# A four-layer transformer block on one core: the sums over a head taken for two states at once on four column tiles, and the decay's second product on two row tiles

## The chip, the core and the metric

The kernel runs on one core of a Trainium2 chip. The metric is the device time in microseconds (us) of one execution, the median of several. Five engines work side by side, each through its own instructions in order: PE (TensorE, the matrix engine, with its weight loads shown apart as PEld), DVE (VectorE), ACT (ScalarE), POOL (GpSimd) and SP (SyncE, which here only issues DMAs). An instruction waits on semaphores for what it needs, and what stands behind it on the same engine waits with it.

## The reference

The input is 32 sequences of 64 tokens with 256 features. Four layers follow each other: a transformer layer with self-attention, cross-attention and an MLP; a recurrent layer (layer 1); a layer with two large cross-attentions of 16 heads of 128 features and an MLP; and a last cross-attention layer. Only layer 1 is touched. Cut to what matters, with 32 heads of 8 features (`h`, `s_`):

```python
xm = xa[:, :, None] + sx[:, :, None] * (maa_stack + xxx)
xk, xw, xv, xr, xg = (xm[:, :, j] for j in range(5))
w = jnp.exp(-jnp.exp(time_decay + jnp.tanh(xw @ td_w1) @ td_w2)).reshape(b, l, h, s_)
r, k, v = ...                      # three 256x256 products of xr, xk, xv
def step(s, rkvw):
    r_t, k_t, v_t, w_t = rkvw
    a = k_t[..., :, None] * v_t[..., None, :]
    out = jnp.einsum('bhi,bhij->bhj', r_t, u * a + s)
    s = a + w_t[..., :, None] * s
    return (s, out)
```

The state `s` of a head is an 8x8 matrix that runs over the 64 tokens. `out` sums over the head's 8 rows. The decay `w` comes from two small products: 256 to 64 features (`td_w1`), a tanh, and 64 to 256 features (`td_w2`).

## The kernel before

**Groups and stages.** The 2048 tokens are four groups of 512 (eight sequences each). A group's activations in layer 1 are tiles of 128 partitions x 2 x 512: 256 features as two halves of 128 partitions (`c` = 0, 1), 512 tokens in the free dimension. Every layer is a Python generator which yields between pieces of work; `weave` runs a main generator and pulls lighter ones along at a rate. Layer 1 of group 0 is a main generator, with layer 0 of group 1 and a filler (the products `k2p_f`, `v2p_f` of layer 2) woven in. Layer 1 of groups 1, 2 and 3 is the light generator, each followed by a layer 0 (or layer 3) of another group, woven at rates 1.13 to 1.25 into layer 2 of the group before. The number of yields of layer 1 therefore sets which piece of layer 2 stands beside which piece of what follows layer 1. The framework then puts every engine's instructions in an order of its own by priority, and adds the waits.

**The recurrence.** `states(c, n)` (L552 to L575) makes the products for two of the eight columns `j` of a head's state, for one half `c`: four calls `n` = 0 to 3 take `j` = (0, 2), (4, 6), (1, 3), (5, 7). In it, a 0/1 matrix spreads `v` over the head's rows with two matmuls (L558, output `vj`), which use two row tiles of the PE array (32 input rows each, `m` = j // 2). DVE multiplies by `k` (L567), then runs two scans over the tokens (L573); POOL writes the start values (L563) and multiplies by `r` (L574). The result is `a`, 128 x 2 x 512.

**The sums over a head.** In the loop at L586 each call's `a` is summed by two matmuls with a 0/1 matrix of 32 columns (L596, output `op`), each on a column tile of 32: tile `m` of `op` gets columns `j` = 2m (`q` = 0, `start`) and `j` = 2m + 1 (`q` = 1, `stop`). So `n` = 0 writes column tiles 0 and 1, `n` = 1 tiles 2 and 3, and `n` = 2, 3 add the odd columns to the same tiles. The loop keeps two calls of `states` ahead. After `n` = 3 a matmul `bp` (L603) and two DVE instructions (L604, L605) finish that half. `beside(i)` gives the second and later matmuls of a set a higher priority, so that they stand behind the first one in PE's order.

**The decay.** `dwp` (through `linear`, L165) is the product with `td_w1`, 64 output columns, on partitions 0 to 63; ACT takes the tanh (L505); `wp` (L510) multiplies by `td_w2`, once for each half `c`, from 64 input rows; ACT takes two exponentials for each half (L512, L513).

**Float32 on PE.** All matmuls are float32, and each is two passes in the trace (64 matmuls of `op` are 128 records).

**Buffers.** `bank` is one of four PSUM tiles of 512 columns, `banks` one of two tiles of 1024 columns, used by `vj`, by layer 2's scores `s2p` and layer 0's scores `sp`. The 128 x 2 x 512 tiles come from a pool of 12 (`four`).

Of the kernel before, what the change touches and what calls it, by code (L numbers as in the profile page):

```python
# [10 lines left out]
AF = mybir.ActivationFunctionType  # L11
# [3 lines left out]
P = 128  # L15
# [6 lines left out]
NC = D // P  # L22
# [5 lines left out]
C_ID, C_HB, C_HB8, C_SEL, C_GAT, C_M0, C_M1 = 0, 128, 256, 384, 640, 704, 705  # L28
# [40 lines left out]
def kernel(  # L69
# [16 lines left out]
    V, A, PL, PE = nc.vector, nc.scalar, nc.gpsimd, nc.tensor  # L86
# [8 lines left out]
    def bank(name):  # L95
        return psum1.tile([P, 512], F32, tag="b1", name=name)
# [20 lines left out]
    ct = cp.tile([P, C_N], F32, name="ct")  # L117
# [13 lines left out]
    def vec(name, i=0):  # L131
        at = VAT[name] + i
        return vt[:, at : at + 1]
# [27 lines left out]
    def linear(ps, w, at, step, y, cols=P):  # L161

        for kc in range(NC):
            o = at + kc * step
            PE.matmul(ps, w[:, o : o + cols], y[:, kc, :], start=(kc == 0), stop=(kc == NC - 1))  # L165
# [259 lines left out]
    @contextmanager  # L425
    def beside(i):

        if i:
            with tc.high_priority(offset=4000):
                yield  # L430
        else:
            yield
# [5 lines left out]
    def cbt(ap):  # L438

        return ap.rearrange("p c (b t) -> p (c b) t", b=GB)  # L440
# [7 lines left out]
    def layer1(g, work):  # L448
# [6 lines left out]
        w5, w6 = slot(L1_AT), slot(L1_AT + 1)  # L455
# [11 lines left out]
        ps = bank(f"t5p_{g}")  # L467
        linear(ps, w5, 0, 192, xx)
        A.activation(t5[:, 0, :], ps, AF.Tanh)
        ps = bank(f"t5bp_{g}")  # L470
# [27 lines left out]
        xw, xk = mixed(1, 0)  # L498
        yield
        yield  # L500
        de = big("de")
        dw = de[:64, 0, :]
        ps = bank(f"dwp_{g}")
        linear(ps[:64, :], w5, 384, 64, xw, cols=64)
        A.activation(dw, ps[:64, :], AF.Tanh)  # L505
        ws = big("ws")
        PL.memset(cbt(ws)[:, :, 0:1], 0.0)
        for c in range(NC):
            ps = bank(f"wp_{g}_{c}")
            PE.matmul(ps, w5[:64, 512 + c * P : 512 + (c + 1) * P], dw, start=True, stop=True)  # L510
            e = de[:, 1, :]
            A.activation(e, ps, AF.Exp, bias=vec("L1_xattn_time_decay", c))  # L512
            A.activation(bt(ws[:, c, :])[:, :, 1:], bt(e)[:, :, :-1], AF.Exp, scale=-1.0)  # L513
        yield

# [2 lines left out]
        for f, n, at in ((0, "k", 0), (2, "v", 512)):  # L518
# [7 lines left out]
            for c in range(NC):  # L526
                ps = bank(f"{n}p1_{g}_{c}")
# [22 lines left out]
        def states(c, n):  # L550

            j0 = (0, 4, 1, 5)[n]  # L552
            vj = banks(f"vj_{g}_{c}_{n}")
            for i in range(2):
                m, q = (j0 + 2 * i) // 2, j0 % 2
                rows = slice(32 * m, 32 * m + 32)
                with beside(i):
                    PE.matmul(  # L558
                        vj[:, i, :], ct[rows, C_SEL + q * P : C_SEL + (q + 1) * P], v[rows, c, :],
                        start=True, stop=True,  # L560
                    )
            a = big(f"a{c}{n}")
            PL.tensor_copy(  # L563
                a.rearrange("p i (b t) -> p i b t", b=GB)[:, :, :, 0:1],
                s0t[:, c, j0 : j0 + 3 : 2, g * GB : (g + 1) * GB].unsqueeze(3),
            )
            V.tensor_tensor(  # L567
                a.rearrange("p i (b t) -> p i b t", b=GB)[:, :, :, 1:],
                vj.rearrange("p i (b t) -> p i b t", b=GB)[:, :, :, :-1],
                bt(k[:, c, :])[:, :, :-1].unsqueeze(1).to_broadcast([P, 2, GB, S - 1]), ALU.mult,  # L570
            )
            for i in range(2):
                V.tensor_tensor_scan(a[:, i, :], ws[:, c, :], a[:, i, :], 0.0, ALU.mult, ALU.add)  # L573
            PL.tensor_tensor(a, a, r[:, c : c + 1, :].to_broadcast([P, 2, GT]), ALU.mult)  # L574
            return j0, a  # L575
# [7 lines left out]
        for c in range(NC):  # L583
            V.scalar_tensor_tensor(ruk[:, c, :], r[:, c, :], vec("L1_xattn_u", c), k[:, c, :], ALU.mult, ALU.mult)
        w9 = slot(L1_AT + 4)
        for at, (c, n) in enumerate(todo):  # L586
            if at + 2 < 8:
                ahead.append(states(*todo[at + 2]))
                yield
            if n == 0:  # L590
                op = bank(f"op_{g}_{c}")
            j0, a = ahead.pop(0)
            for i in range(2):
                m, q = (j0 + 2 * i) // 2, j0 % 2
                with beside(i):
                    PE.matmul(  # L596
                        op[32 * m : 32 * m + 32, :], ct[:, C_GAT + 32 * q : C_GAT + 32 * q + 32], a[:, i, :],
                        start=(q == 0), stop=(q == 1),
                    )
            yield  # L600
            if n == 3:
                bp = bank(f"bp_{g}_{c}")
                PE.matmul(bp, hb, ruk[:, c, :], start=True, stop=True)  # L603
                V.tensor_tensor(v[:, c, :], bp, v[:, c, :], ALU.mult)  # L604
                V.tensor_tensor(v[:, c, :], op, v[:, c, :], ALU.add)  # L605
                yield
# [390 lines left out]
def _layout(inputs):  # L997

    import numpy as np

    f = {k: np.asarray(v) for k, v in inputs.items()}
    i = np.arange(D)
    turned = (i // P) * P + (i % 16) * 8 + (i % P) // 16

    def rows(w):

        return w.reshape(-1, P, w.shape[1]).transpose(1, 0, 2).reshape(P, -1)

    def tall(w):

        return np.concatenate([w, np.zeros((P - w.shape[0], w.shape[1]), w.dtype)], 0)

    def slot(*parts):
        w = np.concatenate(parts, 1)
        return np.concatenate([w, np.zeros((P, WSLOT - w.shape[1]), w.dtype)], 1)

    l0 = {k[9:]: v for k, v in f.items() if k.startswith("L0_xattn_")}
    l1 = {k[9:]: v for k, v in f.items() if k.startswith("L1_xattn_")}
    l2 = {k[9:]: v for k, v in f.items() if k.startswith("L2_xattn_")}
    l3 = {k[9:]: v for k, v in f.items() if k.startswith("L3_xattn_")}  # L1020

    def mlp(w1, w2):

        return [slot(rows(w1[:, :512])), slot(rows(w1[:, 512:])), slot(rows(w2[:512])), slot(rows(w2[512:]))]

    qkv, kv = l0["w_qkv"], l0["w_kv"]
    w2 = l1["maa_w2"]
    maa_w1 = np.concatenate([l1["maa_w1"], l1["maa_w1"][:, 128:]], 1)
    slots = [
        slot(rows(qkv[:, :512])),  # L1030
        slot(rows(qkv[:, 512:]), rows(l0["w_ao"])),
        slot(rows(l0["w_q"]), rows(kv[:, :D])),
        slot(rows(kv[:, D:]), rows(l0["w_co"])),
        *mlp(l0["w1"], l0["w2"]),
        slot(rows(maa_w1), rows(l1["td_w1"]), tall(l1["td_w2"])),
        slot(w2[:4].reshape(P, D), tall(np.concatenate([w2[4], w2[4]], 0))),
        slot(rows(l1["Wk"].T), rows(l1["Wv"].T[:, turned])),
        slot(rows(l1["Wr"].T), rows(l1["Wg"].T[:, turned])),
        slot(rows(l1["Wo"].T[turned]), rows(l1["Wfk"].T)),
        slot(rows(l1["Wfr"].T), rows(l1["Wfv"].T)),  # L1040
    ]
    for a in "12":
        for q in range(4):
            at = slice(512 * q, 512 * q + 512)
            slots += [slot(rows(l2[n + a][:, at])) for n in ("wq", "wk", "wv")]
            slots.append(slot(rows(l2["wo" + a][at])))
    slots += mlp(l2["w_fc1"], l2["w_fc2"])
    slots += [
        slot(rows(l3["q_w"]), rows(l3["k_w"])),
        slot(rows(l3["v_w"]), rows(l3["cproj_w"])),  # L1050
        *mlp(l3["fc_w"], l3["proj_w"]),
    ]
    f["L1_xattn_gn_w"] = l1["gn_w"][turned]
    f["L1_xattn_gn_b"] = l1["gn_b"][turned]

    def feature_major(x):

        return x.reshape(G, GT, NC, P).transpose(3, 0, 2, 1)

    def token_major(x):  # L1060

        return x.reshape(G, TT, P, D).transpose(2, 0, 1, 3)

    ctx = f["ctx_2048"]
    arrays = {
        "x": token_major(f["x"]),
        "cT": feature_major(ctx),
        "s0": ctx[:, 2:10].reshape(B, NC, P, 8).transpose(2, 1, 3, 0),
        "m_self": f["mask_1x1xSxS2_fc1"].reshape(S, S),
        "m_cross": f["mask_Bx1xSxS2_ff1"].reshape(B // 2, 2, S, S).transpose(2, 1, 0, 3),  # L1070
        "m_key": np.ascontiguousarray(f["mask_BxS2_bf1"]).view(np.uint8).reshape(B // 2, 2, S).transpose(1, 0, 2),
        "vecs": np.concatenate([f[n].reshape(-1, P).T for n, _ in VECS], 1),
        "brow": np.concatenate([f[n].reshape(-1) for n in ROWS])[None],
        "vrow": np.stack([np.stack([l2[f"b{v}"].reshape(-1), l2[f"bias_v{a}"].reshape(-1)]) for a, v in (("1", "v1"), ("2", "v2"))]),
        "wts": np.stack(slots),
        "cst": _constants(),
    }
    return {k: np.ascontiguousarray(v) for k, v in arrays.items()}
# [27 lines left out]
```

## Time and profile before

| | |
|---|---|
| median of three runs | 2191.03 us (2188.73 to 2194.2) |
| the profiled execution's own time | 2198.33 us |
| its span, from first to last instruction | 2196.6 us |
| mean granted TensorE clock | 0.973 |
| matmul passes / instructions in the trace | 15264 / 36396 |
| DMA | 197.26 MB, mean 90 GB/s |

In the page a line of a group reads: source line, engine, operation, output and inputs by tile name, shape and type, count, then busy time, mean duration of one in ns, and the idle time of the engine just before, with what ended it. Matmuls are pipelined, so that the durations of single passes overlap; what a set of matmuls really occupies is the distance from its start to the start of the next one. The layer 1 recurrences of the four groups lie at about 313 to 426, 573 to 641, 1005 to 1074 and 1444 to 1520 us of the span.

### The profile page before, as it was taken

What the parts mean: (1) busy time and instruction counts of PE and PEld (TensorE: products, weight loads), DVE (VectorE), ACT (ScalarE), POOL (GpSimd) and SP (SyncE); (2) the same over time, 40 slices, a digit from 0 to 9 for tenths busy, and PEclk for the clock granted to TensorE, in tenths of its full rate; (3) what the DMA queues carried; (4) which work ended last, traced back from release to release, by engine and by line L of the source; (5) the groups of instructions that cost most, each with busy time, mean ns of one, the idle gap of its engine ahead of it and who ended that gap; (6) DMA issues with size and microseconds to landing.
All of it is one profiled execution on the core that took longest, in us unless ns stands there. A gap on an engine that the chain in (4) does not pass through costs nothing. (4 is left out here: it accounts for less than half of the span.)

```text
span 2196.6 us, 36396 instructions
## 1 busy us (share of the span) xinstructions
PE 2058.2 (94%) x15264; PEld 1243.4 (57%) x15264; DVE 1156.9 (53%) x1965; ACT 631.8 (29%) x1000; POOL 542.4 (25%) x498
## 2 busy tenths in 40 slices
PE   5989998999989899999898999999999999999998
PEld 3455444464545565655555656555566767566665
DVE  3672668434655747325548573376574366424662
ACT  1222322223232313232313232322323133321441
POOL 2221344113432313123323131243211111100110
PEclk9999998999999999999999999999999999999998
DMA  7233231237312112333121132331312432212010
GB/s 245 95 128 109 93 104 57 99 106 252 112 58 63 58 47 77 95 112 116 49 63 60 50 100 83 117 123 51 89 55 95 128 121 70 94 43 87 25 39 20
DMA packets 79795, 197.26 MB, mean 90 GB/s; under 512 B 9616, under 2 KB 14352, under 8 KB 79632
## 3 DMA queue, kind: packets, MB, share of 16 engines
q1 hardware_dynamic: 77472, 191.88, 27.2%
q8 instruction: 121, 1.98, 0.4%
q0 software_dynamic: 576, 2.10, 0.3%
q10 hardware_dynamic: 1584, 0.95, 0.1%
q14 instruction: 42, 0.34, 0.1%
HBM read 158.98 MB, written 35.91 MB: 89 GB/s over the span
## 5 line engine op out<-in xcount | busy, mean ns | idle before, releaser
L165 PE MATMUL q2p<-h,w 128*128 128x512 f32 x512 | 245.5, 613 | 7.1 <-DMA w<-in_wts 3.2
L331 PE MATMUL al_o<-w,o 128*128 128x256 f32 x1024 | 235.6, 388 | 11.7 <-DVE o L836 10.7
L331 PEld LDWEIGHTS al_o<-w,o 128*128 128x128 f32 x1024 | 196.9, 194 | 53.3 <-issue 17.6
L786 ACT ACTIVATE q<-q2p,vt 128x512 f32<-128x512 f32 x128 | 87.3, 685 | 284.1 <-PE q2p L165 281.6
L165 PEld LDWEIGHTS q2p<-h,w 128*128 128x128 f32 x512 | 95.4, 194 | 123.0 <-issue 104.9
L804 POOL TENSOR_TENSOR pn<-s,sm 128x512 f32<-128x512 f32 x64 | 72.3, 1132 | 288.9 <-DVE sm L209 206.6
L165 PE MATMUL k2p_f<-c,w 128*128 128x512 f32 x256 | 130.0, 629 | 5.3 <-DMA w<-in_wts 3.3
L734 PE MATMUL v2p_f<-w,c 128*128 128x512 f32 x256 | 122.8, 602 | 0.0
L734 PE MATMUL v2p<-w,c 128*128 128x512 f32 x256 | 118.1, 604 | 2.4 <-ACT pt_b L290 1.3
L165 PE MATMUL k2p<-c,w 128*128 128x512 f32 x256 | 120.0, 593 | 0.0
L945 DVE TENSOR_TENSOR fv<-v2p_f,vb 128x512 f32<-128x512 f32 x64 | 43.8, 686 | 114.9 <-PE v2p_f L734 114.9
L574 POOL TENSOR_TENSOR a<-a,r 128x1024 f32<-128x1024 f32 x32 | 75.7, 2366 | 113.2 <-DVE a L573 99.9
L344 DVE TENSOR_TENSOR x<-al_o,x 128x512 f32<-128x512 f32 x64 | 43.7, 684 | 100.4 <-PE al_o L331 100.4
L836 DVE TENSOR_SCALAR o<-pv,vt 128x256 f32<-128x256 f32 x128 | 55.8, 473 | 74.9 <-PE pv L825 74.6
L936 ACT ACTIVATE fk<-k2p_f,vt 128x512 f32<-128x512 f32 x64 | 44.0, 687 | 172.1 <-PE k2p_f L165 142.1
L772 DVE TENSOR_SCALAR k<-k2p,vt 128x512 f32<-128x512 f32 x64 | 47.3, 744 | 86.3 <-PE k2p L165 86.3
L796 PEld LDWEIGHTS s2p<-k,q 128*64 128x64 f32 x2048 | 67.9, 138 | 42.4 <-issue 30.5
L825 PEld LDWEIGHTS pv<-pt,v 64*64 64x64 f32 x4096 | 72.7, 140 | 26.1 <-issue 17.7
L734 PEld LDWEIGHTS v2p_f<-w,c 128*128 128x128 f32 x256 | 50.1, 196 | 63.8 <-issue 62.4
L200 DVE TENSOR_REDUCE mx<-s2p 128x8 f32<-128x520 f32 x64 | 44.4, 694 | 78.2 <-PE s2p L796 78.0
L825 PE MATMUL pv<-pt,v 64*64 64x64 f32 x4096 | 81.6, 226 | 3.2 <-issue 1.4
L165 PEld LDWEIGHTS k2p<-c,w 128*128 128x128 f32 x256 | 48.9, 191 | 61.3 <-issue 57.9
(310 smaller groups left out, 3733.3 us busy)
## 6 DMA issues: line engine op xcount, KB each, us to landing
w<-in_wts SPq DMA_DIRECT2D x200, 512.0 KB, 3.6
kd<-fk SPq DMA_DIRECT2D x64, 260.0 KB, 2.1
k<-kd SPq DMA_DIRECT2D x64, 260.0 KB, 3.9
vd<-fv SPq DMA_DIRECT2D x64, 256.0 KB, 2.0
v<-vd SPq DMA_DIRECT2D x64, 256.0 KB, 4.3
vb<-in_vrow SPq DMA_DIRECT2D x20, 256.0 KB, 4.1
vs<-in_vrow SPq DMA_DIRECT2D x20, 256.0 KB, 3.4
c<-in_cT POOLq DMA_DIRECT2D x4, 512.0 KB, 11.6
```

Of the source, the lines that this page charges most:

```text
L165: PE.matmul(ps, w[:, o : o + cols], y[:, kc, :], start=(kc == 0), stop=(kc == NC - 1))
L200: V.tensor_reduce(mx, src, AX.X, ALU.max)
L331: PE.matmul(ps[:, a, :], y[kc][:, i * P : (i + 1) * P], wk[:, o : o + D], start=(kc == 0), stop=(kc == k - 1),)
L574: PL.tensor_tensor(a, a, r[:, c : c + 1, :].to_broadcast([P, 2, GT]), ALU.mult)
L734: PE.matmul(ps, cs[g][:, kc, bp * P : (bp + 1) * P], wv[:, 512 * kc : 512 * kc + 512], start=(kc == 0), stop=(kc == NC - 1),)
L772: V.tensor_scalar_add(k[:, :, :S], bt(ps), vec(f"L2_xattn_bk{a}", hd))
L786: A.activation(q, ps, AF.Identity, bias=vec(f"L2_xattn_bq{a}", hd))
L796: PE.matmul(sp[64 * h2 : 64 * h2 + 64, b // 4, (b % 4) * (S + 1) : (b % 4 + 1) * (S + 1)], qs[h2][:, b * S : (b + 1) * S], ks[h2][:, b, :] ...
L804: PL.tensor_tensor(pn, s[:, :, :S], rc.unsqueeze(2).to_broadcast([P, GB, S]), ALU.mult)
L825: PE.matmul(pv[b2][rows, to : to + S], vals[bp][half, hc : hc + 64], pt[half, bp, h2 * S : (h2 + 1) * S], start=True, stop=True,)
L836: V.tensor_scalar_add(ov[:, :, 1, :], src[1], bv)
L936: A.activation(k[:, :, :S], bt(ps), AF.Identity, bias=vec("L2_xattn_bk1", hd))
```

## The change

The head sums of two calls of `states` are made together: four matmuls on four column tiles, in one step of the loop instead of two. Two calls of `states` are still kept ahead. Where a step does not finish a half, a yield stands in the place of the `bp` step; the loop yields 14 times instead of 16. For the decay, `td_w1` is stored twice side by side, so that `dwp` has 128 output columns and the tanh stands twice, on partitions 0 to 63 and 64 to 127; `td_w2` is stored with its first 128 columns on partitions 0 to 63 and its last 128 on partitions 64 to 127, and the two `wp` matmuls read one half of the rows each (two row tiles), into two banks that are taken together.

```diff
         de = big("de")
-        dw = de[:64, 0, :]
+        dw = de[:, 0, :]
         ps = bank(f"dwp_{g}")
-        linear(ps[:64, :], w5, 384, 64, xw, cols=64)
-        A.activation(dw, ps[:64, :], AF.Tanh)
+        linear(ps, w5, 384, P, xw)
+        A.activation(dw, ps, AF.Tanh)
         ws = big("ws")
         PL.memset(cbt(ws)[:, :, 0:1], 0.0)
-        for c in range(NC):
-            ps = bank(f"wp_{g}_{c}")
-            PE.matmul(ps, w5[:64, 512 + c * P : 512 + (c + 1) * P], dw, start=True, stop=True)
+        wps = [bank(f"wp_{g}_{c}") for c in range(NC)]
+        for c in range(NC):
+            rows = slice(64 * c, 64 * c + 64)
+            with beside(c):
+                PE.matmul(wps[c], w5[rows, 640 : 640 + P], dw[rows], start=True, stop=True)
+        for c in range(NC):
             e = de[:, 1, :]
-            A.activation(e, ps, AF.Exp, bias=vec("L1_xattn_time_decay", c))
+            A.activation(e, wps[c], AF.Exp, bias=vec("L1_xattn_time_decay", c))
             A.activation(bt(ws[:, c, :])[:, :, 1:], bt(e)[:, :, :-1], AF.Exp, scale=-1.0)
         yield
...
         w9 = slot(L1_AT + 4)
-        for at, (c, n) in enumerate(todo):
-            if at + 2 < 8:
-                ahead.append(states(*todo[at + 2]))
+        for at in range(0, 8, 2):
+            c, q = todo[at][0], at // 2 % 2
+            for nxt in todo[at + 2 : at + 4]:
+                ahead.append(states(*nxt))
                 yield
-            if n == 0:
+            if q == 0:
                 op = bank(f"op_{g}_{c}")
-            j0, a = ahead.pop(0)
-            for i in range(2):
-                m, q = (j0 + 2 * i) // 2, j0 % 2
-                with beside(i):
+            two = [ahead.pop(0)[1] for _ in range(2)]
+            for m in range(4):
+                with beside(m):
                     PE.matmul(
-                        op[32 * m : 32 * m + 32, :], ct[:, C_GAT + 32 * q : C_GAT + 32 * q + 32], a[:, i, :],
-                        start=(q == 0), stop=(q == 1),
+                        op[32 * m : 32 * m + 32, :], ct[:, C_GAT + 32 * q : C_GAT + 32 * q + 32],
+                        two[m // 2][:, m % 2, :], start=(q == 0), stop=(q == 1),
                     )
             yield
-            if n == 3:
+            if q == 0:
+                yield
+            else:
                 bp = bank(f"bp_{g}_{c}")
...
     maa_w1 = np.concatenate([l1["maa_w1"], l1["maa_w1"][:, 128:]], 1)
+    td_w1 = np.concatenate([l1["td_w1"], l1["td_w1"]], 1)
...
-        slot(rows(maa_w1), rows(l1["td_w1"]), tall(l1["td_w2"])),
+        slot(rows(maa_w1), rows(td_w1), l1["td_w2"].reshape(64, NC, P).transpose(1, 0, 2).reshape(P, P)),
```

## The prediction

> **What bounds the kernel now.** I read the page's first part, the windows of the four recurrences, and then PE's timeline inside one of them.
>
> ```profile
> PE 2058.2 (94%) x15264; PEld 1243.4 (57%) x15264; DVE 1156.9 (53%) x1965; ACT 631.8 (29%) x1000; POOL 542.4 (25%) x498
> ...
> core 0: us, PE busy (x) PEld busy (x) DVE busy (x) ACT busy (x) POOL busy (x), PEclk, DMA share, GB/s
> 313.00:426.00 113.00, 102.99 (x535) 48.08 (x534) 80.16 (x100) 27.04 (x42) 39.95 (x35) 0.94 0.23 82
> 573.00:641.00 68.00, 60.97 (x518) 33.59 (x518) 45.67 (x55) 14.51 (x25) 26.01 (x16) 0.95 0.29 87
> 1005.00:1074.00 69.00, 61.96 (x519) 34.22 (x518) 45.79 (x55) 14.27 (x24) 25.94 (x15) 0.93 0.29 86
> 1444.00:1520.00 76.00, 73.62 (x739) 42.33 (x732) 50.67 (x63) 22.58 (x36) 27.17 (x16) 1.00 0.24 78
> ```
>
> PE is busy for 2058 of 2197 us, so PE work taken away shortens the end wherever PE is not about to wait. The windows tell where it is: in the recurrences of groups 0, 1 and 2 PE idles 10, 7 and 7 us while DVE is 66 to 71% busy, in group 3 only 2.4 us. Next PE's timeline in group 1 (start, duration with the overlapping tails, engine, line; the bracket is idle time and what ended it):
>
> ```profile
> 581.97 1.14 PE L558 MATMUL vj<-v,ct 32*128 32x512 f32 x8
> 583.04 0.66 PE L810 MATMUL tp<-ct,pn 128*128 128x128 f32 x4
> 583.62 1.05 PE L596 MATMUL op<-a,ct 128*32 128x512 f32 x4
> 584.61 0.66 PE L810 MATMUL tp<-ct,pn 128*128 128x128 f32 x4
> 585.19 1.16 PE L825 MATMUL pv<-pt,v 64*64 64x64 f32 x64
> 586.28 1.13 PE L558 MATMUL vj<-v,ct 32*128 32x512 f32 x4
> 587.34 1.16 PE L825 MATMUL pv<-pt,v 64*64 64x64 f32 x64
> 589.35 1.05 PE L596 MATMUL op<-a,ct 128*32 128x512 f32 x4 [0.84 <-POOL a L574]
> 590.33 1.13 PE L558 MATMUL vj<-v,ct 32*128 32x512 f32 x4
> 592.36 1.10 PE L331 MATMUL al_o<-w,o 128*128 128x256 f32 x4 [0.90 <-PE vj L558]
> 596.64 5.59 PE L331 MATMUL al_o<-w,o 128*128 128x256 f32 x17 [3.18 <-DVE o L836]
> ```
>
> From start to next start, a pair of head sums (four passes) occupies PE for 0.98 to 0.99 us (583.62 to 584.61, 589.35 to 590.33). The first line is the one that matters most: eight passes of `vj` on four row tiles take 581.97 to 583.04, 1.07 us, where four passes on two row tiles take 586.28 to 587.34, 1.06 us. So four tiles side by side cost no more than two. The last line shows the other side: there PE waits for DVE.
>
> **The change, part by part.** All against the profiled execution's 2198.3 us.
>
> *Head sums.* 32 pairs become 16 sets of four: 4 groups x 8 pairs x 0.98 = 31.4 us before. A set of four column tiles of 512 columns has no row. It costs at least a pair, 0.98, and at most two pairs, 1.96. The nearest rows are `vj` (same 512 columns, four row tiles, 1.07 against 1.06) and `pv_b`, four column tiles of only 64 columns:
>
> ```profile
> L298 PE MATMUL pv_b<-pt_b,vb 128*32 128x64 f32 x512 | 10.5, 231 | 1.9 <-DVE fv L945 1.0 <-issue 0.8
> ```
>
> 10.5/512 is 20.5 ns a pass, 82 ns for four; a single pass of 64 columns would be 57 ns, an estimate by a quarter of al_o's 0.23 (235.6/1024). That is 1.44 passes for four, or 0.98 x 1.44 = 1.41 us a set; but passes so short are nearer to PE's rate of issue, so I take `vj`: 1.00. Saved 16 x (1.96 - 1.00) = 15.4; by `pv_b` 16 x 0.55 = 8.8; at worst 0.
>
> A rule that speaks against this stands in the Trainium skill, "TensorE: Matmul & The Clock Gate", Part 3, measured speedup: three column tiles of 512 columns brought 2.38x and four row tiles 3.07x, not 3x and 4x. By 4/3.07 = 1.30 of a lone matmul, an estimate from that page, a set would cost 1.28 us and the 16 sets would save 10.9 us; this trace's `vj` shows no such loss from two tiles to four.
>
> *The decay.* Two `wp` matmuls, four passes one after the other, become two passes on two row tiles.
>
> ```profile
> 541.04 1.98 PE L510 MATMUL wp<-de,w 64*128 64x512 f32 x4
> ...
> 542.95 0.68 PE L796 MATMUL s2p<-k,q 128*64 128x65 f32 x14
> ```
>
> 541.04 to 542.95 is 1.91; after, 1.06 as a pair of `vj`. Saved 3 x 0.85 in groups 1 to 3, and about 1.0 in group 0, where it takes 2.69 (254.67 to 257.36): 3.6 together, bounds 0 to 4.2. `dwp` keeps its four passes; its output now fills all columns, which drops a change of tiling beside other full-width matmuls (0.52 instead of 0.43 us between starts in the trace): 0.3. The tanh has twice the partitions and the same 512 columns: ACT takes 584 ns for a 128x512 copy and 590 for the 64x512 tanh, so nothing, and ACT is 29% busy. Doubled weights change no DMA: the slot stays 512 KB.
>
> *`vj` meets `vj`.* Two calls of `states` now stand before a step, and in the built program's order their four spreads stand together once more in each of groups 0, 1, 2 and 3. Four tiles in one go save 1.06 each if both `banks` are free: 0 to 4.2. I count 2.1 (groups 1 and 2; in 0 and 3 DVE has not read the first bank yet).
>
> Gross: 15.4 + 3.6 + 0.3 + 2.1 = 21.4.
>
> *New waits.* A set needs two states, and in PE's queue everything behind it waits too: layer 2's `pv`, `al_o`, `s2p`, and through them DVE. A state takes 1.21 (multiply), 2.34 (two scans) and 2.36 us (POOL), with waits 6.3 from the end of `vj` (583.04) to POOL's end (586.94 + 2.36 = 589.30). I walk group 1 with its own rows. The set now stands after the first `pv` block; PE gets there at about 587.1 and must wait for 589.3, 2.2 us where 0.84 stood. `al_o` still waits for DVE's evictions to 596.6, so nothing gained by then counts. From there PE runs ahead until the last set: its second state needs DVE and POOL until about 625.3, PE arrives at 621.7. Past that set and the score block behind it PE is at 628.0 with what it had done at 631.4: 3.4 gained of 4 x 0.96 + 1.06 = 4.9, so 1.5 lost, in group 2 the same. In group 0 two sets lie before waits for DVE that already exist (1.41 and 2.65 us for `s_b` after the pairs at 343.5 and 355.4): 2.0 lost. Group 3, nearly without idle: 1.0, between 0 and 3.8. Together 6.0.
>
> *Two yields fewer.* What follows layer 1 comes two steps earlier. Before, the last products of layer 0 or 3 (`al_c`, `al_j`) stood between `nt_h` and `h_h` and covered the eviction of the norm; in the new order they come before `nt_h`. Where no cover stands, the critical chain shows the price:
>
> ```profile
> 2158.56 1.74 PE nt_j L190 x7
> ...
> 2160.33 0.82 DVE y_j L192
> 2161.15 0.04 issue
> 2161.20 16.97 PE h_j L165 x32
> ```
>
> 0.87 between the two products, three times: 2.6. All other meetings of layer 2 with layer 0 and 3 shift too; I set that at 0 with 8 us to either side (PE idles 20 us in 641 to 900 and 19 in 1074 to 1340, where they meet).
>
> Net: 21.4 - 6.0 - 2.6 = 12.8, say 13: 2185.3 for an execution like the profiled one. That one lies 7.3 above the median; the same gain on the median of 2191.0 gives 2178.
>
> **Rivals.** *Everything counts* (chance 0.2): PE is the bound throughout, the waits are absorbed, all `vj` sets merge: 21.4 + 2.1 = 23.5 less a few us, 2170. For it: 94% busy. Against: al_o's 3.18 wait for DVE.
>
> *The sums were not the bound* (0.18): in groups 0 to 2 DVE and POOL set the pace and each set waits for its second state; their part of the net, 11.5 of head sums + 2.1 - 5.0 = 8.6, goes: 2187. The same time comes if four column tiles don't run side by side (the change doesn't do what it says): 15.4 less in the gross, against which the sets would wait less (6.0): 2187. Against the latter: the `vj` and `pv_b` rows.
>
> *The shifted meeting costs* (0.12), the slower side: at 4.8 us a time PE waited for DVE's `s_a` at layer 0's transposes (`tp_a`), once each in groups 2 and 3. With two steps less between softmax and transposes such a wait could come at every second of the eight softmaxes of each of those two layers, six more times: 6 x 4.8 = 29, less 13 = 16 slower, 2207. From three such waits on the gain is gone. For it: DVE is 60% busy there. Against: the order keeps layer 2's products between them.
>
> **How the numbers follow.** The forecast, 2178, has 0.5 (its own range 2167 to 2185, from 24 gained to 6); the rivals 0.2, 0.18, 0.12. A difference below 0.3%, 6.6 us, can't be told from none. Faster by more than that: 0.5 + 0.2 = 0.70. Within: 0.18 of the second rival plus 0.01 = 0.19. Slower: 0.11. The range that leaves out 2 in 10 goes from 2164 to 2196.
>
> **What would show it.** Right: `op` still 128 records with some 17 us busy instead of 33.8; eight passes of `op` from start to next start in 1.0 us; `wp` 1.06; PE's busy time 2036 to 2040. Wrong: 1.4 to 2 us for a set; PE's waits for POOL `a` (5.9 us now) above 15; idle time of PE above 150 us (138 now), in 641 to 900 above all.

## The result: slower, and where it went in the profile after

| | before | after |
|---|---|---|
| median, the two run in turn | 2191.84 us (2188.73 to 2194.2, 6 runs) | 2211.31 us (2204.22 to 2213.8, 6 runs) |
| ratio, 95% interval | | 1.0082 [1.0065, 1.01] |
| profiled execution, its span | 2198.33, 2196.6 us | 2212.12, 2210.3 us |
| PE idle (span less busy) | 138.4 us | 162.7 us |
| time at granted TensorE clock 0.5 (1 is full speed) | 120.1 us | 142.2 us |

The kernel became 0.82% slower, 18 us, where 13 us of gain were forecast. The profiled execution of before lies 6.5 us above its median, that of after 0.8 us, so the two profiles differ by some 6 us less than the medians. First the page's busy times and the windows of the four recurrences (start and end, length, busy time of each engine with its count, granted clock, DMA):

```profile
PE 2047.6 (93%) x15264; PEld 1239.4 (56%) x15264; DVE 1157.1 (52%) x1965; ACT 637.9 (29%) x1006; POOL 537.7 (24%) x498
```

```profile
306.00:416.00 110.00, 100.03 (x543) 46.91 (x542) 82.14 (x107) 28.53 (x44) 43.08 (x37) 0.95 0.25 82
564.00:632.00 68.00, 56.68 (x469) 32.14 (x468) 47.93 (x54) 14.41 (x23) 23.45 (x15) 0.92 0.27 84
997.00:1066.00 69.00, 57.65 (x470) 32.41 (x469) 48.06 (x55) 14.98 (x24) 23.44 (x15) 0.93 0.27 84
1438.00:1511.00 73.00, 66.37 (x664) 39.09 (x665) 52.08 (x66) 21.59 (x34) 27.13 (x17) 1.00 0.24 80
```

PE is busy 10.6 us less and idles 24 us more. In the windows of the recurrences of groups 1 and 2 it now idles 11 of 68 and 69 us, before 7. The two edits themselves, from PE's timeline (start, duration, engine, line, operation; the bracket is idle time and what ended it):

```profile
531.18 1.13 PE L512 MATMUL wp<-de,w 64*128 64x512 f32 x4
532.24 0.68 PE L801 MATMUL s2p<-k,q 128*64 128x65 f32 x14
```

```profile
601.00 1.07 PE L599 MATMUL op<-a,ct 128*32 128x512 f32 x8
601.99 1.15 PE L801 MATMUL s2p<-k,q 128*64 128x65 f32 x32
...
615.02 1.05 PE L599 MATMUL op<-a,ct 128*32 128x512 f32 x4
619.71 1.92 PE L599 MATMUL op<-a,ct 128*32 128x512 f32 x4 [3.63 <-POOL a L577]
621.56 1.11 PE L815 MATMUL tp<-ct,pn 128*128 128x128 f32 x4
```

`wp` takes 1.06 us from start to next start, as forecast. A set of four head sums in one piece (eight passes at 601.00) takes 0.99, the price of one pair before. But the set at 615.02 is not one piece: PE starts the two matmuls of the first state, then stands 3.63 us for the second state. That happens to 5 of the 16 sets: the first and the last of groups 1 and 2, the last of group 3. PE's wait for the states doubles by it (us in total, times, longest; first before, then after):

```profile
PE op L596 <- POOL a L574: 5.9, 4, 2.1
```

```profile
PE op L599 <- POOL a L577: 11.2, 5, 3.6
```

The large loss lies elsewhere. The table follows five marks through the profiled executions of nine kernels of the study: the first matmul of `nt_f`, the norm ahead of the first of layer 2's two attentions, in each of the four groups, and, at 2088 us of before, the first matmul of the last `nt_i`, a norm of layer 3. It gives what each stretch between marks took against before, in us; the middle three are layer 2 of groups 0, 1 and 2. "Ends" is how far the last mark has moved.

| | to 517 | 517 to 952 | 952 to 1383 | 1383 to 1753 | to 2088 | ends |
|---|---|---|---|---|---|---|
| after | -11.2 | +2.9 | +2.1 | +21.1 | +0.4 | +15.3 |
| e1_sixteen | -10.9 | 0.0 | -5.7 | -3.4 | +0.3 | -19.7 |
| e2_fourteen | -7.4 | -0.7 | -1.3 | +24.1 | +0.5 | +15.2 |
| e4_sums | -12.4 | +0.4 | +1.0 | +24.1 | +0.4 | +13.5 |
| e5_rates | -10.5 | -4.5 | -5.7 | -3.8 | +2.0 | -22.5 |
| e6_third | -11.8 | +2.7 | +2.1 | -4.0 | -1.3 | -12.3 |
| e7_firsttwo | -15.5 | -1.1 | -1.9 | +21.6 | +0.4 | +3.5 |
| e8_act_evict | -11.0 | +2.9 | +1.8 | +19.3 | +2.2 | +15.2 |
| e12_fifteen | -8.9 | -5.7 | -7.1 | +2.3 | -1.6 | -21.0 |

Each row is one execution, and executions of one kernel differ by several us and more (those of e12_fifteen lie between 2169.4 and 2187.5 us), so that only the 20 us in one column stand out. After is 11 us ahead when layer 2 begins and 6 us ahead at 1383. It loses 21 us in layer 2 of group 2, beside which the recurrence of group 3 and then layer 3 of group 0 are woven. PE's waits in the second half of this stretch (1530 to 1768 us in after, 1534 to 1753 before), from the list of waits, first after, then before:

```profile
PE h_h L165 <- DVE hm L192: 6.8, 1, 6.8
PE tp_i L289 <- DVE s_i L279: 3.9, 1, 3.9
PE h_j L165 <- ACT hm_j L352: 2.1, 1, 2.1
PE q2p L165 <- DVE h L192: 1.3, 1, 1.3
```

```profile
PE q2p L165 <- DVE h L192: 2.0, 1, 2.0
PE v2p L734 <- DVE x L344: 1.1, 1, 1.1
PE vp_i L242 <- DVE vb L254: 1.0, 1, 1.0
```

Three waits are new, 12.8 us, all in the part with layer 3 of group 0. Around each of them the granted clock is 0.5 for a while (from 1599.1 for 6.8 us, 1677.6 for 3.4, 1735.7 for 6.8), where before has no such stretch between 1383 and 1753. That is 17 us, of which 4 lie in the waits themselves. In the other 13 passes start further apart (those of `h_h` 0.85 us instead of 0.43), so up to 6.5 us are lost there: with the waits 19, nearly the whole loss. How the longest wait arises is seen in the timeline of after, PE and the DVE lines that matter:

```profile
1716.23 7.07 PE L331 MATMUL al_o<-w,o 128*128 128x256 f32 x32
...
1723.14 7.07 PE L331 MATMUL al_j<-w,hm_j 128*128 128x256 f32 x32
...
1730.05 1.04 PE L190 MATMUL nt_h<-ct,xn_h 128*128 128x128 f32 x8
...
1732.15 2.12 DVE L177 TENSOR_SCALAR rs_i<-mv_i 128x4 f32<-128x4 f32 x1
...
1735.47 1.06 DVE L180 TENSOR_SCALAR xn_i<-x,mv_i,rs_i 128x256 f32<-128x256 f32 x3 [1.20 <-POOL rs_i L178]
1736.44 0.68 DVE L356 TENSOR_TENSOR x<-al_j,x 128x512 f32<-128x512 f32 x1
1737.04 0.80 DVE L192 TENSOR_SCALAR hm<-nt_h,vt 128x512 f32<-128x512 f32 x1
...
1737.90 2.93 PE L165 MATMUL h_h<-hm,w 128*128 128x512 f32 x3 [6.82 <-DVE hm L192]
```

and the same place before:

```profile
1717.62 1.04 PE L190 MATMUL nt_h<-ct,xn_h 128*128 128x128 f32 x8
...
1718.50 7.07 PE L331 MATMUL al_j<-w,hm_j 128*128 128x256 f32 x32
...
1723.25 0.80 DVE L192 TENSOR_SCALAR hm<-nt_h,vt 128x512 f32<-128x512 f32 x1
1725.41 7.03 PE L165 MATMUL h_h<-hm,w 128*128 128x512 f32 x16
```

The eviction `hm` takes 0.80 us in both. In after it stands in DVE's queue behind `rs_i` and `xn_i`, the norm of another group's layer 3, which itself waits for POOL, and behind the addition of `al_j`. Before, 7 us of `al_j` on PE covered this, and DVE had finished 1.4 us before PE came.

### The profile page after: what moved, and what is told of

It is laid out like the page before. It is cut to its first block, busy times and chain, and to the rows that moved or that the text cites. A ratio compares the mean times of both kernels' runs of the same rounds, so it can differ in the third digit from the quotient of the medians.

```text
span 2210.3 us, 36423 instructions
## 1 busy us (share of the span) xinstructions
PE 2047.6 (93%) x15264; PEld 1239.4 (56%) x15264; DVE 1157.1 (52%) x1965; ACT 637.9 (29%) x1006; POOL 537.7 (24%) x498
## 5 line engine op out<-in xcount | busy, mean ns | idle before, releaser
L809 POOL TENSOR_TENSOR pn<-s,sm 128x512 f32<-128x512 f32 x64 | 67.6, 1057 | 318.1 <-DVE sm L209 234.5
L576 DVE TENSOR_TENSOR_SCAN a<-ws,a 128x512 f32<-128x512 f32 x64 | 86.5, 1387 | 2.3
L739 PEld LDWEIGHTS v2p<-w,c 128*128 128x128 f32 x256 | 48.3, 197 | 62.1 <-issue 46.0
```

The lines of the kernel that those rows point to most:

```text
L739: PE.matmul(ps, cs[g][:, kc, bp * P : (bp + 1) * P], wv[:, 512 * kc : 512 * kc + 512], start=(kc == 0), stop=(kc == NC - 1),)
L809: PL.tensor_tensor(pn, s[:, :, :S], rc.unsqueeze(2).to_broadcast([P, GB, S]), ALU.mult)
```

## The experiments

Theory A: the two missing yields shift what follows layer 1 against layer 2, and that costs more than the packed matmuls save. Theory B: the sets of four cost it, by waiting for their second state. Medians stand beside those of the kernel before in the same batch: 2193.49 us for e1, e2, e3 and e5, 2193.59 for e4, e6, e7 and e8, 2192.09 for e9 to e12.

**e1_sixteen**: the changed kernel, with the number of yields put back.

```diff
                 V.tensor_tensor(v[:, c, :], op, v[:, c, :], ALU.add)
                 yield
+                yield
```

> The changed kernel with a second yield after each half's bp step, so that layer 1's loop yields 16 times again and its light chain ends at layer 2's step 82 of 90, not 80. Theory A (the two missing yields moved the end of the light chain off the norm of layer 2's MLP and shifted every meeting; the packed matmuls themselves save): 2171 to 2181 us, 10 to 20 below before's 2191.8; PE's idle time back to about 138 us from 163, the 6.8 us wait of h_h gone. Theory B (the sets of four wait for their second state and cost more than they save): above 2200 us, PE's wait for POOL a still 11 us.

Measured 2183.5 us (7 runs), ratio 0.9955 [0.9938, 0.9972]. Against the changed kernel that is 0.0127, 28 us. The order was the loss; with the old number of yields the two edits, both still there, are together a gain.

**e2_fourteen**: the kernel before, pairs and old decay, with two yields less.

```diff
-            yield
+            if n != 0:
+                yield
             if n == 3:
```

> The kernel before without the yield after the first sum of each half: pairs as before, decay as before, 14 yields in the loop. Theory A: 2205 to 2225 us, since only the meetings are those of the changed kernel and no matmul is saved. Theory B: 2192 us within 5.

2212.27 us (4 runs), ratio 1.0094 [1.0074, 1.0113]. The order alone, with none of the change's matmuls, costs 0.0094, 20.6 us, and the table has its loss in the same stretch. Theory B can't explain it.

**e3_decay**: only the decay's part of the diff on the kernel before (the head sums stay pairs, 16 yields).

> The decay part alone on the kernel before (16 yields): both theories 2187 to 2190 us, 2 to 5 below before (wp 1.06 instead of 1.91 us in three groups, some 1 us more in group 0). If the decay part were the cost, above 2196.

2188.95 us (10 runs), ratio 0.9979 [0.9962, 0.9996]: 4.6 us saved, from 0.9 to 8.3. In e1_sixteen the head sums on four column tiles bring 0.0024 more, 5.3 us, at the edge of what the two intervals can tell apart.

**e4_sums**: only the sums' part (14 yields, old decay).

> The sums over a head of the change alone; the decay is as before, layer 1 yields 14 times per group. If the loss is the shifted order (theory A), this carries all of it, and only the decay's gain (4.5 us as the decay alone gave against its kernel before) is missing: 2213 to 2217, with the half-clock time near 140 us again. If the new decay itself does something harmful in the changed order (two banks taken together), this is below the changed kernel: 2200 or less.

2216.33 us (4 runs), ratio 1.0095 [1.0073, 1.0118]. The whole loss comes with the sums' part and its two missing yields, as expected; but the half-clock time was 125 us, not near 140. Beside e2_fourteen (1.0094) the packing itself shows no gain in this order, while it shows 5.3 us with 16 yields. The cause of that stays open, and the intervals overlap.

**e5_rates**: the changed kernel; layer 1 keeps 14 yields, but is pulled along more slowly, so that what follows it again meets layer 2 about where it did. The rates of the chains that begin with layer 1 of groups 1, 2 and 3 are the second to fourth of the list: 1.13, 1.13 and 0.93 steps for each step of layer 2, not 1.13 to 1.25; 1.25 is the rate of layer 0 of group 1 beside layer 1 of group 0.

```diff
-RATES = (1.25, 1.13, 1.13, 0.93, 0.46, 1.6)
+RATES = (1.25, 1.10, 1.10, 0.905, 0.46, 1.6)
```

> The changed kernel with the light chains' rates lowered from 1.13, 1.13, 0.93 to 1.10, 1.10, 0.905, so that they end at layer 2's step 82 of 90 again, with 14 yields in the loop. Theory A: 2172 to 2186 us, a little above e1 because the meetings inside the chain are stretched evenly and not put back. Theory B: above 2200 us.

2179.55 us (4 runs), ratio 0.9947 [0.9927, 0.9967]. A second way to about the old meeting, with no step added, brings back 0.0135, 29.6 us.

**e6_third** and **e7_firsttwo** split this by place.

```diff
-RATES = (1.25, 1.13, 1.13, 0.93, 0.46, 1.6)
+RATES = (1.25, 1.13, 1.13, 0.905, 0.46, 1.6)    e6_third
+RATES = (1.25, 1.10, 1.10, 0.93, 0.46, 1.6)     e7_firsttwo
```

> The changed kernel with only the third rate changed, 0.93 to 0.905, so that in layer 2 of group 2 alone the steps of layer 3 group 0 stand where they stood before. Theory A in its narrow form (most of the loss is this one stage: 14 us of idle and 17 us of half clock): 20 to 24 us come back, 2187 to 2192, and the matmul that ends the stage (nt_h of group 2) lies 20 us earlier while all stages before it keep their times. Its rival (the loss is the same in each of the three weaves): one third of the 32 us that all three rates brought, 2198 to 2203.

> The changed kernel with the first two rates changed, 1.13 to 1.10, and the third left. Narrow theory A: only the two stages around layer 2 of groups 0 and 1 recover (by the stage table 6 + 17 and 8 + 15 us against what the start of the chain gives back), together 8 to 16 us: 2195 to 2203. Rival (equal shares): two thirds of 32 us, 2188 to 2192. The two kernels of this pair together should give the 32 us of all three rates; more or less than that would mean that the stages are not independent.

e6_third: 2183.63 us (5 runs), ratio 0.9943 [0.9922, 0.9965], 30.5 us back where 20 to 24 were expected. e7_firsttwo: 2202.95 us (5 runs), 1.0046 [1.0031, 1.0061], 7.9 back. The third rate alone recovers nearly all. In the table after and e6_third part in the stretch 1383 to 1753, by 25 us, and by less than 2 in every other; e7_firsttwo keeps its +21.6 there and gains 4 in each of the two stretches before. The medians' sum, 38, is more than the 29.6 of e5_rates, at the edge of what the intervals (about 4 us each) allow, so that it stays open whether the stages are independent. PE's list of waits for e6_third in the same half of the stretch (1530 to 1742 us) has none of the three:

```profile
PE al_o L331 <- DVE x L344: 1.2, 1, 1.2
PE vp_i L242 <- DVE vb L254: 1.0, 1, 1.0
```

and the two windows from 1566 us to the end of the stage (first after, then e6_third) say it in sums: 201.4 us at clocks 0.96 and 0.95 against 175.7 at 1.00.

```profile
1566.50:1663.80 97.30, 92.42 (x898) 59.28 (x897) 59.46 (x97) 25.64 (x47) 13.90 (x15) 0.96 0.22 66
1663.80:1767.90 104.10, 95.18 (x634) 64.29 (x633) 31.00 (x69) 28.07 (x40) 15.51 (x14) 0.95 0.31 97
```

```profile
1566.30:1656.00 89.70, 87.52 (x926) 57.13 (x925) 59.73 (x98) 24.83 (x46) 13.75 (x18) 1.00 0.19 60
1656.00:1742.00 86.00, 85.75 (x589) 59.82 (x590) 29.37 (x68) 25.13 (x37) 15.71 (x11) 1.00 0.40 117
```

**e8_act_evict**: the changed kernel; the late eviction `hm` of `nt_h` in group 2 goes from DVE to ACT.

```diff
-            if c == 0:
+            if c == 0 and nm != "h2":
```

> The changed kernel, PE's order untouched; the first half of the norm nt_h2 (layer 2, group 2, the MLP's) is evicted by ACT instead of DVE, where it stood behind the norm of layer 3 group 1 and the addition of al_j. If that queue is the cause of the 6.8 us wait of h_h, the wait falls to 1.5 to 2 us and the half-clock stretch of 6.8 us behind it goes or halves: 5 us of idle and up to 3.4 us of clock, 2203 to 2206. If PE would wait there for something else anyway (ACT's own queue, or the bank), no change: 2209 to 2213.

2210.2 us (4 runs), ratio 1.007 [1.0051, 1.0089]: no change. The timeline says why:

```profile
1731.64 1.98 PE L165 MATMUL h_h<-hm,w 128*128 128x512 f32 x4 [0.43 <-ACT hm L194]
...
1736.58 0.68 DVE L356 TENSOR_TENSOR x<-al_j,x 128x512 f32<-128x512 f32 x1
...
1737.31 2.93 PE L165 MATMUL h_h<-hm,w 128*128 128x512 f32 x3 [3.69 <-DVE x L356]
```

`h_h` now starts 6.3 us earlier, runs its first product, and then waits 3.69 us for `x<-al_j`, another instruction in the same DVE queue behind the same `rs_i`. By the program PE's next product needs a bank of the same pool of four that `al_j` is in, which is why it can wait for this addition; the trace names only the addition. So the second branch of the expectation came: at this place PE needs two results out of DVE's queue, and the eviction was only one of them. The 2 us won at the mark of 1753 are gone at the last mark, in a stretch that has 3.4 us more of half clock.

**e9_late** and **e10_both**: 16 yields, the extra ones placed so that the split sets come later. **e11_14** does the same within the 14 yields and rates of e5_rates, by moving the yield behind the first and the last set ahead of it.

```diff
+            if at == 6:             e9_late
+                yield
+                yield
+            if at in (0, 6):        e10_both, e11_14
+                yield
             two = [ahead.pop(0)[1] for _ in range(2)]
```

> The changed kernel with 16 yields again, but the two extra ones stand ahead of the last set of head sums instead of after the two halves. In the changed kernel 5 of 16 sets fell apart into two pairs because the second state came late, the last set of groups 1, 2 and 3 and the first of groups 1 and 2. If that is why the packed sums give 5 us where 11.5 were forecast, the last sets of groups 1 and 2 run in one piece here, PE's wait for POOL a falls from 6.9 (16 yields after the halves) to about 3.5, and the time is 3 to 4 us below that kernel's: 2179 to 2181. If the wait only moves (what follows layer 1 then waits for DVE and POOL), the same as there: 2182 to 2186.

> 16 yields, one extra ahead of the first set and one ahead of the last set of each group. By the same reasoning both the first and the last sets find their second state one step earlier in its making: 0 to 2 of 16 sets split, PE's wait for POOL a 2 to 5 us, 2178 to 2181. If one step (2 to 3 us of other work) is too little for the last set (it waited 2.3 to 3.6 us), it still splits and the time is that of the kernel with 16 yields after the halves: 2182 to 2186.

> 14 yields with all three rates lowered (that kernel stood at 0.9947 of before), and the first and last set of each group one step later within them (the yield behind each of these sets now stands ahead of it). If sets that split cost what their waits show (4.6 us there), 2 to 4 us below that kernel: ratio 0.993 to 0.994, 2176 to 2180. If the first and last sets are not what PE waits for in the end, the same: 0.9945 to 0.995.

e9_late 2181.14 us (4 runs), 0.9952 [0.9935, 0.9968]; e10_both 2183.5 (7 runs), 0.9959 [0.9946, 0.9972]; e11_14 2178.43 (7 runs), 0.994 [0.9924, 0.9957]. None can be told from e1_sixteen or e5_rates. The first and last sets of groups 1 and 2 stay split in all three, which the edits were to prevent. e9_late's time lies where it was expected, but not for the reason given: PE's wait for POOL `a` rose to 8.4 us instead of falling to 3.5. In e11_14 it is 4.1 us, in e5_rates 4.6. In e10_both this wait falls, and the next ones take its place (e1_sixteen first, then e10_both; the `issue` row is the wait of `al_o` at the same place in group 1):

```profile
PE al_o L331 <- DVE o L842: 8.7, 4, 4.5
PE op L599 <- POOL a L577: 6.9, 4, 2.3
...
PE al_o L331 <- issue: 4.5, 1, 4.5
```

```profile
PE al_o L331 <- DVE o L843: 11.2, 4, 6.7
PE al_o L331 <- issue: 6.6, 1, 6.6
...
PE op L601 <- POOL a L577: 4.4, 4, 2.0
```

In sum 20.1 and 22.2 us: what the sets wait less, `al_o` waits more. This fits a pace set by DVE and POOL at these places in groups 1 and 2, so that where PE waits for it makes no difference.

**e12_fifteen**: one of the two missing yields put back, behind the first half only.

```diff
                 V.tensor_tensor(v[:, c, :], op, v[:, c, :], ALU.add)
                 yield
+                if c == 0:
+                    yield
```

> The changed kernel with one of the two missing yields put back (15). In PE's order both al_j still stand ahead of nt_h of group 2, as in the changed kernel, while in groups 0 and 1 one of the two al_c covers again. Theory A with the place named by the third rate alone (the cover between nt_h and h_h, and the softmax of layer 3 group 0 beside layer 2): most of the 25 us stays, 2200 to 2210. Its rival (the cost grows evenly with the number of yields missing): half of it, 2195 to 2199.

2179.49 us (9 runs), ratio 0.9941 [0.9924, 0.9959]: all of it back, against both expectations. One step decides, not an even price per yield. And `h_h` hardly waits, although nothing stands between `nt_h` and `h_h` here either:

```profile
1683.35 7.07 PE L331 MATMUL al_o<-w,o 128*128 128x256 f32 x32
...
1690.25 13.98 PE L331 MATMUL al_j<-w,hm_j 128*128 128x256 f32 x64
...
1704.06 1.04 PE L190 MATMUL nt_h<-ct,xn_h 128*128 128x128 f32 x8
...
1705.07 0.80 DVE L192 TENSOR_SCALAR hm<-nt_h,vt 128x512 f32<-128x512 f32 x1
1705.93 14.00 PE L165 MATMUL h_h<-hm,w 128*128 128x512 f32 x32 [0.83 <-DVE hm L192]
```

So the cover has to be counted from `al_o`, whose sum the norm needs, and not from `nt_h`. From the end of `al_o` (1723.1 in after) DVE needs until 1737.8 for the statistics, both norms and the eviction: 14.7 us. PE has 7 us of `al_j` and 1 of `nt_h` to put there in after, where one half of `al_j` has slipped ahead of `al_o`. It has 14 and 1 in e12_fifteen, and as much before, where one half stands on each side of `nt_h`. 14.7 less 8 is about the wait of 6.8. That the shifted meeting is the cause is shown by the runs with the step or the rate put back. That this one queue is the largest part of it is read from the traces: no run removes that wait alone, and what `tp_i` and `h_j` waited for was not followed up in the same way.

## Why the prediction was wrong, point by point

- **A set of four for the price of a pair**: right. 0.97 to 1.00 us from start to next start for a set in one piece, taken as 1.00 from `vj`; neither 1.41 by `pv_b` nor the estimate of 1.28 came. But only 11 of 16 sets run in one piece, which brings 11 x 0.97 = 10.7 instead of 15.4; `op` is busy 24.0 us, not 17, and PE 2047.6 us, not 2036 to 2040.
- **The decay**: right. `wp` 1.06 in groups 1 to 3; 1.41 instead of 2.69 in group 0. 4.6 us measured alone, 3.9 forecast.
- **`vj` beside `vj`**: eight passes run in one piece 6 times instead of 3, the new ones in groups 1, 2 and 3: 3 x 1.06 = 3.2 where 2.1 was counted. In group 0 the spreads stand together too, but PE waits 1.36 us for DVE between them, much as the prediction held for it. Two further waits of `vj`, 0.7 us each in groups 1 and 2, are new.
- **New waits of the sets**: named in the right place and near in size. PE's wait for POOL `a` went from 5.9 to 11.2 us. Together with the splits, the head sums bring 5.3 us (e1_sixteen against e3_decay) where 15.4 + 2.1 - 6.0 = 11.5 stood.
- **Two yields fewer**: the step that failed. It stood at 2.6, as three evictions of 0.87, and "All other meetings of layer 2 with layer 0 and 3 shift too; I set that at 0 with 8 us to either side". It measured 20.6 us alone (e2_fourteen) and 28 within the change (e1_sixteen against it). The 0.87 holds where only the eviction is uncovered: two waits of `h_h` in groups 0 and 1 sum to 1.3 us, and e12_fifteen has 0.83. In group 2 it was 6.8, because the price was taken from a place at the end of the program where DVE has nothing else to do, and here DVE's queue held another group's norm. The waits of `tp_i` and `h_j` and the half clock around all three make the rest of what that stretch lost. Which instructions of DVE stand between was in the trace of before (its order at 1718 to 1725) and in the new order of PE, and was not walked as group 1's recurrence was.
- **The rivals**: the one on the slower side had about the time, 2207, but its place was layer 0's transposes, and PE's wait `tp_a` even fell, 12.8 to 11.0 us. What came was a softmax wait of layer 3 (`tp_i`), once, and mostly the norm ahead of the MLP. That the rival's time was near is luck. Of the rival by which the sums were not the bound a part came: in groups 1 and 2 the last set splits in e1, e5 and e9 to e12 too.
- **The sign of being wrong**: PE's idle time, 162.7 us, is above the 150 named, but not in 641 to 900 above all. Of the new idle time 16.7 us lie between the marks 1383 and 1753, 4.5 and 5.4 in the two stretches before.
- **The range** ended at 2196, with the unknown meeting bounded by 8 us; alone it measured 20.6. The 8 us were set beside the idle time of 641 to 900 and 1074 to 1340. The loss came in the third stage, 1520 to 1760, which was not named and where PE idled only 5 us before: little idle time is no bound on a new wait. With about the old meeting, the same matmuls give 2178.4 to 2183.6 us (e1, e5, e6, e9 to e12), 9 to 13 us faster than before: the net of the other terms, where 21.4 - 6.0 = 15.4 stood.

## What to carry to other kernels

Where streams are interleaved by counting steps, taking a step out is an edit of everything that follows: count what each stream meets, and put the step or the rate back before judging the edit itself. To price a wait, start from the instruction whose result is needed first, add up all that stands in the slower engine's queue from there, and compare it with PE's work over the same stretch; the one instruction that the wait names is only its end. A change that merges two steps of a pipeline needs its inputs sooner; see whether the second one is ready before counting the merged price.

## What the runs showed of the hardware

- Four column tiles of 512 columns take the time of two: 0.97 to 1.00 us for eight passes in after, 0.98 for four before; the second four passes of a set start 0.45 us after the first four. The matmuls of a set wait one by one, so that a set whose second half is late runs as two pairs (615.02 and 619.71 in after), at the price of two.
- The granted clock falls to 0.5 in stretches nearly all of 3.4 or 6.8 us (27 of 28 in after). The three in the lost stage lie on waits of PE of 2.1 to 6.8 us, so a wait there cost more than its length: 12.8 us of waits, up to 6.5 on top. Not every wait has one: the same wait of `al_o` for DVE, 2.7 us ahead of 1822.7 in after, of 1807.8 before and of 1820.8 in e8_act_evict, is followed by 3.4 us at 0.5 in the last two and by none in after. In the profiled executions the sum of such stretches runs from 97.9 us (e1_sixteen) to 145.7 (e8_act_evict). It also differs where the order is the same: up to the mark of 517 us after has 27.3 us of it and e7_firsttwo 17.1. Half of the difference, 5.1, is about the 4.3 us between the two at that mark.
